# CIN head on one core: M's tile rows read ahead of chunk 4, chunk 4's loads and products threaded between the last two, and the first pair's operands ahead of two weight sums

## The chip, the cores and the metric

The kernel runs on one core of one Trainium2 chip. The metric is the device time of one launch in microseconds (us). All data are float32.

## The reference

A compressed interaction network (CIN) with three layers over x of shape (B, F, E) = (1024, 64, 16), pooled over E and reduced to one number per batch row:

```python
x0 = h = x; xs = []
for i in range(3):                       # W0, W1, W2: 128 output channels each
    z = einsum('bfe,bge->bfge', x0, h)   # all products of two features
    y = einsum('oc,bce->boe', W[i], z.reshape(B, -1, E)) + b[i][None, :, None]
    x_i, h = (y[:, :64], y[:, 64:]) if i < 2 else (y, y)
    xs.append(x_i)
out = concatenate(xs, axis=1).sum(axis=2) @ fc_w.T + fc_b     # (1024, 1)
```

The output is linear in the last layer, so the kernel never forms layer 2 (or the kept half of layer 1) in full. It contracts W2 with fc_w beforehand, and with W1 it builds a small matrix, called M in this text, that maps products of x with x to a weighted sum.

## The kernel before

**Tiling.** The batch is cut into 32 chunks of 32 rows; a chunk is x transposed to features on partitions and N = 32*16 = 512 columns. The host lays out two copies: `xa` (128 partitions, four shifted windows, 1 MB a chunk) and `xb` (four tiles of 256 KB, `xb[c][0..3]`, each a shift of the features). A *product* `z[c, j] = xa[c] * xb[c][j]` (128 x 2048) holds four of the 16 tiles of all pairs of features; the index j is called the tile row. 16 tiles, t = 4j + i, times the matching weight tiles `w_all[:, t]` give one chunk's result in PSUM. `w_all[:, t, 0:64]` are the layer-0 weights (from W0), `w_all[:, t, 64:128]` the M weights.

**Where M comes from.** `m_sb` is computed on TensorE, written to a DRAM scratch tile `md` (L428 to L434), and read back skewed: `read_rows` (L479) and `read_columns(j)` (L473) fill the block `ms`, and `q_weights(j)` (L506, VectorE) adds the two parts into `w_all` for tile row j. A column read is made of 256-byte pieces.

**Order of the head.** Chunks 2, 3, 0, 1 (in this order) form the head. `half_contract` (L262) makes their layer-0 half while M is under way. Then `head_q_tile` (L280) multiplies chunks 0 and 1 with the M weights: 16 tiles in order of t, so tile rows j = 0, 1, 2, 3 in turn. After that TensorE contracts chunk 4 (16 tiles) and chunk 5 (14 of 16), does some small matmuls on squares and sums of x (`v0x`, `h_extra`, `q_extra`), and enters the pairs.

**Pairs.** From chunk 6 on, chunks go in pairs (12 of them, `NPAIR`), each pair with fewer matmul tiles by a Winograd-like scheme. Its operands are `B22`, `T3`, `X`, `B21` (VectorE products, `w_product`, L657), `w_both` (L663, adds two xb tiles), and `T2` and its successors (GpSimd differences, `w_mix`, L672). They use weight sums `ws` (L524 to L529) which are made from `w_all` on GpSimd and ScalarE. The window of a pair begins on TensorE with `alpha` from X and `delta` from T3.

**Lists and queues.** Every engine runs its instructions in program order. From L537 on, the program order is that of a list: `at(when, fn, ...)` records a call, and the list is sorted by `when` at the end (one unit is about one TensorE tile of 0.86 us; `when = 0` is chunk 4's first tile, `t = T0 = 33` the first pair's window). Before the change everything up to L534, the whole of `head_q_tile` among it, stands ahead of that list. `load_xa`, `load_xb` issue from the SyncE queue (SPq). Each xb tile that VectorE multiplies is first copied into PSUM by ScalarE (`second`, L577; two banks, tag "y"). GpSimd multiplies three products itself with xb from SBUF: (4, 3), (5, 2), (5, 3). `weigh`, `add_up`, `place` (L560, L564, L569) scale W1's and W0's kept halves by fc_w on GpSimd, sum them on VectorE and put the columns in place on ScalarE. Fourteen blocks `z0..z13` are handed out in the order in which they came free (`take`, `used`).

A DMA signals one of a few semaphores; before one of these is used again, the earlier DMA on it must have landed.

Of the kernel before, what the change touches and what calls it, by code (L numbers as in the profile page):

```python
# [38 lines left out]
AF = mybir.ActivationFunctionType  # L39
ALU = mybir.AluOpType  # L40
# [10 lines left out]
NI = 4  # L51
NJ = 4
NT = NI * NJ
# [4 lines left out]
KEPT = HEAD[-2:]  # L58
NV = 200
SQ = slice(96, 128)  # L60
# [8 lines left out]
def cin_kernel(ctx, tc, xra, xrb, wh, w0r, w1h, w2t, wx1, wx0, vec, out):  # L69
    nc = tc.nc  # L70
# [6 lines left out]
    halves = [slice(0, F), slice(F, 128)]  # L77

    def const_tile(name, shape):
        return const.tile(shape, F32, tag=name, name=name)  # L80
# [4 lines left out]
    def take(uses=1):  # L85
        n = vacant.pop(0)
        left[n] = uses
        return n

    def used(n, times=1):  # L90
        left[n] -= times
        assert left[n] >= 0
        if left[n] == 0:
            vacant.append(n)
# [9 lines left out]
    w0ds, fcr = vs[:, 8:72], vs[:, 72:200]  # L104
# [25 lines left out]
    w_all = const_tile("w_all", [128, NT, 128])  # L130
    ws = const_tile("ws", [128, 5, 2 * NI, F])
    va, vb, v0 = (const_tile(n, [128, F]) for n in ("va", "vb", "v0"))
# [8 lines left out]
    def load_xa(c, at=slice(0, NI)):  # L141
        if c not in xas or at.start == 0:
            xas[c] = xp.tile([128, NI, N], F32, tag="xa", name=f"xa_{c}")
        nc.sync.dma_start(
            out=xas[c][:, at, :],
            in_=bass.AP(
                tensor=xra.tensor, offset=c * XR * N + at.start * N,
                ap=[[N, 128], [1, (at.stop - at.start) * N]],
            ),
        )  # L150

    def quarter(c, j):
        xbs.setdefault(c, {})[j] = xp.tile([128, N], F32, tag="xb", name=f"xb_{c}_{j}", bufs=9)
        return xbs[c][j]

    def load_xb(c, *js):
        for j in js or range(NJ):
            nc.sync.dma_start(out=quarter(c, j), in_=xrb[c, :, j, :])
# [74 lines left out]
    def new_acc(c, n=N, tag="acc"):  # L233
        if c == NCH - 1:
            parts[c] = [
                (ps.tile([128, cols.stop - cols.start], F32, tag=tag, name=f"acc_{c}_{n}", bufs=bufs), cols)
                for n, (tag, bufs, cols) in enumerate(
                    (("acc", 4, slice(0, E * CUT)), ("set", 2, slice(E * CUT, N)))
                )
            ]  # L240
            return
        accs[c] = ps.tile([128, n], F32, tag=tag, name=f"acc_{c}", bufs=4 if tag == "acc" else 2)
# [34 lines left out]
    def head_q_tile(k, j, i):  # L277
        t = j * NI + i
        for c in (2 * k, 2 * k + 1):
            nc.tensor.matmul(  # L280
                accs[c][halves[1 - c % 2]], w_all[:, t, 64:128], blocks[zs[c, j]][:, i, :],
                start=(t == 0), stop=False, skip_group_check=True,
            )
            used(zs[c, j])
# [97 lines left out]
    for h in range(2):  # L382
        at = slice(32 * h, 32 * h + 32)
# [38 lines left out]
    def m_ap(f1, f2, dims):  # L422
        return bass.AP(tensor=md.tensor, offset=md.offset + f1 * row + f2 * F, ap=dims)
# [12 lines left out]
        in_=m_rows[0:4, 4 * F :].rearrange("p (k c) -> p k c", c=4 * F),  # L436
    )
    used(mb)
    load_xa(4, slice(0, 2))

    for j in (0, 1):
        xb3 = ps.tile([128, N], F32, tag="y", name=f"xp_{c3}_{j}")
# [18 lines left out]
    msb = take()  # L461
    ms = flat(msb).rearrange("p (v t g) -> p v t g", v=2, g=F)

    def skewed(f1, f2, dims):

        at = len(dims) - 2
        return m_ap(f1, f2, dims[:at] + [[row + F, F]] + dims[at:])
# [4 lines left out]
    def read_columns(j, queue, half):  # L472
        queue.dma_start(  # L473
            out=ms[halves[half], 1, j * NI : (j + 1) * NI],
            in_=skewed(0, 16 * half + 4 * (j + 1), [[row, NI], [1, F]]),
        )

    def read_rows(js, queue, half):
        queue.dma_start(  # L479
            out=ms[halves[half], 0].rearrange("p (j i) g -> p j (i g)", i=NI)[:, js],  # L480
            in_=skewed(
                16 * half + 4 * (js.start + 1), 0, [[4 * row, js.stop - js.start], [1, NI * F]]
            ),
        )

    for half, queue in enumerate(queues):
        read_rows(slice(0, 1), queue, half)
        read_columns(0, queue, half)
        read_rows(slice(1, NJ), queue, half)
    load_xa(4, slice(2, NI))  # L490


    new_acc(c3, H2)
# [2 lines left out]
    keep_h1(c2)  # L496
    half_contract(c3, 0, 3, 1, 2, last=2)

    for j in range(1, NJ):
        for half in range(2):  # L500
            read_columns(j, nc.scalar if half and j == 2 else nc.sync, half)
    nc.sync.dma_start(out=va[halves[1]], in_=m_ap(0, 0, [[row + F, F], [1, F]]))

    def q_weights(j):
        at = slice(j * NI, (j + 1) * NI)
        nc.vector.tensor_tensor(w_all[:, at, 64:128], ms[:, 0, at], ms[:, 1, at], ALU.add)  # L506
# [2 lines left out]

    for j in range(NJ):
        q_weights(j)
    used(msb)
    nc.vector.memset(w_all[SQ, (NJ - 1) * NI, 64:128], 0.0)


    load_xb(4)
    for c in KEPT:
        new_acc(c, tag="set")  # L520
    for t in range(NT):
        head_q_tile(0, t // NI, t % NI)

    nc.gpsimd.tensor_tensor(ws[:, 2], w_all[:, 0:8, 0:64], w_all[:, 0:8, 64:128], ALU.subtract)  # L524
    nc.gpsimd.tensor_tensor(ws[:, 1], ws[:, 0], w_all[:, 0:8, 64:128], ALU.add)
    nc.gpsimd.tensor_tensor(ws[:, 3], w_all[:, 8:16, 64:128], ws[:, 1], ALU.subtract)
    nc.gpsimd.tensor_tensor(vb[halves[1]], va[halves[1]], w0ds[halves[1]], ALU.subtract)
    nc.scalar.activation(ws[:, 4], w_all[:, 8:16, 0:64], AF.Identity, scale=-1.0)
    nc.scalar.activation(ws[:, 4, NI], ws[:, 2, NI], AF.Identity, scale=-1.0)  # L529

    cst = const_tile("cst", [128, 1])

# [6 lines left out]
    def at(when, fn, *args, **flags):  # L539
        ops.append((when, len(ops), fn, args, flags))  # L540
# [39 lines left out]
    def plain_product(when, c, j):  # L580
        at(when - 2.6, second, c, j)
        at(when, product, c, j, uses=NI)
# [193 lines left out]
    def load_pair(t, p, b0, a0, b1, a1):  # L776
        a, b = p["a"], p["b"]
        at(t + b0, load_xa, b)
        at(t + b0, load_xb, b, 2, 0)
        at(t + a0, load_xa, a)  # L780
        at(t + a0, load_xb, a, 0)
        at(t + b1, load_xb, b, 3, 1)
        at(t + a1, load_xb, a, 1, 2, 3)
        for c in (b, a):
            at(t + 1, load_e, c)
            at(t + 14, square, c)
        at(t + 1.1, load_xx, p["k"])


    T0 = 33  # L790
    at(-7, load_chunk, 5)
    at(-0.2, load_wx, 0, wx0)
    at(-0.1, load_wx, 1, wx1)
    at(-1.5, copy_x, 4)
    at(4.5, copy_x, 5)
    for v, fc, mul, add, put in ((0, fcr[:, 0:64], 4, 17, 17.1), (1, fcr[:, 64:128], 5, 20, 20.1)):
        at(mul, weigh, v, fc)
        at(add, add_up, v)
        for vw in (va, vb) if v else (v0,):
            at(put, place, v, vw, QS if v else 1.0)  # L800
    for j in range(NJ - 1):
        plain_product(-6.5 + 3 * j, 4, j)
    for j in range(2):
        plain_product(4 + 2.6 * j, 5, j)
    for when, c, j in ((-6, 4, 3), (2, 5, 2), (3, 5, 3)):
        at(when, product, c, j, engine=nc.gpsimd, uses=NI)
    for k in (0, 2):
        at(-0.6, new_y, k, "acc")
# [14 lines left out]
    for c in (4, 5):  # L823
        at(T0 + 19.5, factors, c)
    at(T0 + 19.6, sums, 2, slice(0, 128), slice(0, 1))


    pairs = []
    for n in range(NPAIR):
        k = n + 3  # L830
        s = k % 2
        p = {
            "k": k, "A": halves[s], "O": halves[1 - s], "b": 2 * k + s, "a": 2 * k + 1 - s,
            "late": 1 + n % 2 if n else 0,
        }
        pairs.append(p)
        t = T0 + SPAN * n
        if n == 0:
            load_pair(t, p, -39.9, -33.3, -33.15, -27)
            make_pair(  # L840
                t, p, (-23.4, -20.7, -20.4, -17.8, -14.2, -11.5, -8.1, -7, -4, 3),
                (-5, -4.9, 7.2, 12.4, 16.4, 21.7),
            )
            left5 = [[(contract_half, 5, 3, i, n) for i in (2, 3)] for n in range(2)]
            window(
                t, p, ([left5[1][0], (q_extra, 4, va)], [left5[1][1]]),
                [left5[0][0], (q_extra, 5, va), None, None], [left5[0][1], None],
                GROUPS,
            )
        else:  # L850
            q = pairs[-2]
            load_pair(t, p, -34, -28, -27.8, -27.7)
            make_pair(
                t, p, (-21.4, -18.7, -18.4, -15.8, -12.2, -9.5, -6.1, -2, 1.6, 4.2),
                (-5, 2.8, 7.2, 12.4, 16.4, 21.7),
            )
            window(t, p, (first_fill(q), second_fill(q)), late_run(q))
            end_pair(t, q, (0.7, 11.7, 17.9, 22.3, 23.2, 24, 27.5))
# [45 lines left out]
    c, k = NCH - 1, NP - 1  # L904
    t, q = T0 + SPAN * NPAIR, pairs[-1]
    for n, when in ((2, t - 34), (3, t - 29), (c - 1, t - 12), (c, t - 3)):
# [150 lines left out]
```

## Time and profile before

| | |
|---|---|
| median of 5 runs | 468.26 us (464.82 to 470.85) |
| the profiled execution | 468.26 us, of which 466.5 us are the span from the first to the last instruction |
| granted TensorE clock, mean | 0.996 |
| TensorE busy | 457.1 us (98%) |
| VectorE busy | 398.4 us (85%) |
| GpSimd busy | 330.3 us (71%) |
| ScalarE busy | 119.1 us (26%) |
| DMA | 86.04 MB, 184 GB/s over the span |

In a timeline line the columns are: start in us, length in us, engine, line of the kernel, operation, output<-input, the count of merged instructions, and in brackets the idle time of the engine just before, with what ended it. In the chain of waits a line is start, length, and what the end of the program was waiting for at that moment. PE is TensorE, DVE VectorE, ACT ScalarE, POOL GpSimd, SPq the queue of SyncE. TensorE records two matmuls for each float32 matmul, 0.43 us each at 512 columns.

### The profile page before, as it was taken

To read this page: it belongs to the slowest core of one execution; us is meant where nothing else is said; L and a number is where in the kernel's file an instruction comes from. 1 tells how busy PE (TensorE), PEld (TensorE's weight loads), DVE (VectorE), ACT (ScalarE), POOL (GpSimd) and SP (SyncE) were. 2 spreads that over 40 slices of the span, in tenths; PEclk is the share of its full clock that TensorE was granted. 3 is DMA by queue.
4 is the path that set the end of the run, shared out by engine and by line. 5 is a ranking of instruction groups with operands and counts; after the bars stand their busy time and mean duration, and the time that the engine had idled before them with its cause. 6 is when DMAs were issued, how large, how long until landed. Compare 5 with 4: busy or idle time off the path is not lost.

```text
span 466.5 us, 6048 instructions
## 1 busy us (share of the span) xinstructions
PE 457.1 (98%) x2308; PEld 169.0 (36%) x2308; DVE 398.4 (85%) x283; ACT 119.1 (26%) x219; POOL 330.3 (71%) x99
## 2 busy tenths in 40 slices
PE   7999899998999999999999999999999999999997
PEld 4565243332333333333333333333333333244444
DVE  4994897999798989989898998989898998999621
ACT  2162331241313113131213113131312214222111
POOL 5322789596898979899798979899798979500000
PEclk9999999998999999999999999999999999999999
DMA  7998896393728174553719274472818565061000
GB/s 300 415 288 223 284 413 259 138 299 123 262 53 307 58 250 155 181 215 129 278 35 301 83 242 162 141 253 91 288 44 281 165 204 191 16 210 36 0 0 2
DMA packets 32752, 86.04 MB, mean 184 GB/s; under 512 B 6128, under 2 KB 6800, under 8 KB 27924
## 3 DMA queue, kind: packets, MB, share of 16 engines
q1 hardware_dynamic: 31668, 84.64, 53.0%
q10 hardware_dynamic: 1056, 1.02, 0.9%
q8 instruction: 18, 0.29, 0.2%
q14 instruction: 10, 0.08, 0.1%
HBM read 84.00 MB, written 1.64 MB: 184 GB/s over the span
## 4 chain that ended last, share of the span: by engine, by line
PE 90%; DMA 4%; DVE 2%; SPq 2%; issue 1%; ACT 1%; ACTq 0%; DVEq 0%
PE alpha L549 53%; PE acc L549 16%; PE delta L549 8%; PE beta L549 7%; PE acc L262 2%; PE acc L280 2%; DMA z<-md 2%; DMA z<-in_w0r 2%; DVE z L657 1%; DMA md<-z 1%; PE y L549 1%; SPq L433 1%; SPq L432 0%; PE pm L399 0%; PE pv L372 0%
## 5 line engine op out<-in xcount | busy, mean ns | idle before, releaser
L672 POOL TENSOR_TENSOR z<-z,z 128x2048 f32<-128x2048 f32 x72 | 286.6, 4016 | 38.0 <-PE alpha L549 32.8
L657 DVE TENSOR_TENSOR z<-xa,xp 128x2048 f32<-128x2048 f32 x96 | 216.7, 2280 | 15.3 <-POOL z L672 13.7
L549 PE MATMUL alpha<-z,ws 128*64 128x512 f32 x576 | 196.6, 593 | 0.0
L549 PE MATMUL delta<-z,ws 128*64 128x512 f32 x336 | 152.2, 600 | 0.0
L577 ACT COPY xp<-xb 128x512 f32<-128x512 f32 x93 | 54.6, 588 | 207.2 <-DVE z L657 170.3
L549 PEld LDWEIGHTS alpha<-z,ws 128*64 128x64 f32 x576 | 61.6, 137 | 106.1 <-issue 105.9
L549 PE MATMUL beta<-z,w_all 128*64 128x512 f32 x216 | 96.9, 593 | 0.0
L549 PE MATMUL alpha<-z,w_all 128*64 128x512 f32 x192 | 88.6, 605 | 2.2 <-DVE z L657 2.0
L549 PE MATMUL acc<-z,w_all 128*64 128x512 f32 (+3 forms) x320 | 77.2, 509 | 0.0
L248 DVE TENSOR_TENSOR z<-xa,xp 128x2048 f32<-128x2048 f32 (+2 forms) x33 | 67.6, 2087 | 4.3 <-ACT xp L577 1.6
L549 PEld LDWEIGHTS delta<-z,ws 128*64 128x64 f32 x336 | 45.1, 138 | 9.1 <-issue 9.1
L549 PEld LDWEIGHTS alpha<-z,w_all 128*64 128x64 f32 x192 | 25.8, 139 | 61.3 <-issue 49.5
L549 PEld LDWEIGHTS acc<-z,w_all 128*64 128x64 f32 (+1 forms) x320 | 32.3, 148 | 35.8 <-issue 35.4
L549 PEld LDWEIGHTS beta<-z,w_all 128*64 128x64 f32 x216 | 29.0, 137 | 14.0 <-issue 14.0
L262 PE MATMUL acc<-z,w_all 128*64 128x256 f32 x256 | 29.1, 382 | 1.9 <-DVE z L248 1.7
L248 POOL TENSOR_TENSOR z<-xa,xb 128x2048 f32<-128x2048 f32 x4 | 18.2, 4558 | 16.4 <-DMA xb<-in_xrb 16.4
L262 PEld LDWEIGHTS acc<-z,w_all 128*64 128x64 f32 x256 | 17.9, 137 | 14.2 <-DVE z L248 3.6
L549 PE MATMUL delta<-z,w_all 128*64 128x512 f32 x48 | 22.6, 592 | 0.0
L298 DVE SCALAR_TENSOR_TENSOR uu<-acc,vs,snap 64x512 f32<-64x512 f32 (+2 forms) x5 | 3.2, 643 | 20.1 <-ACT snap L291 20.1
L307 DVE TENSOR_REDUCE acc<-uu 128x64 f32<-128x1024 f32 (+3 forms) x20 | 20.2, 1016 | 0.2
L663 DVE TENSOR_TENSOR xp<-xp,xb 128x512 f32<-128x512 f32 x24 | 16.8, 698 | 0.7
L179 ACT ACTIVATE e<-e 64x512 f32<-64x512 f32 x28 | 16.1, 621 | 4.1 <-DMA e<-in_xra 3.9
(101 smaller groups left out, 297.5 us busy)
## 6 DMA issues: line engine op xcount, KB each, us to landing
xb<-in_xrb SPq DMA_DIRECT2D x128, 256.0 KB, 6.8
xa<-in_xra SPq DMA_DIRECT2D x31, 1024.0 KB, 5.3
e<-in_xra SPq DMA_DIRECT2D x28, 128.0 KB, 4.1
xx<-in_xra SPq DMA_DIRECT2D x28, 128.0 KB, 2.5
z<-in_w2t SPq DMA_DIRECT2D x2, 1024.0 KB, 10.8
z<-in_wx SPq DMA_DIRECT2D x2, 1024.0 KB, 9.4
xa<-in_xra SPq DMA_DIRECT2D x3, 512.0 KB
z<-in_w1h SPq DMA_DIRECT2D x1, 1024.0 KB
```

The source lines that it names most:

```text
L179: nc.scalar.activation(es[c][halves[1]], es[c][halves[0]], AF.Square)
L248: engine.tensor_tensor(blocks[zs[c, j]][:, at, :], xas[c][:, at, :], xbs[c][j].unsqueeze(1).to_broadcast([128, last - first, N]), ALU.mult,)
L262: nc.tensor.matmul(accs[c][halves[n]], w_all[:, t, 0:64], blocks[zs[c, j]][:, i, n * H2 : (n + 1) * H2], start=(t == 0), stop=(j == last a ...
L280: nc.tensor.matmul(accs[c][halves[1 - c % 2]], w_all[:, t, 64:128], blocks[zs[c, j]][:, i, :], start=(t == 0), stop=False, skip_group_chec ...
L298: nc.vector.scalar_tensor_tensor(uu[h, 0, cols], acc_c[h], bh1[h], q, ALU.add, ALU.mult)
L307: nc.vector.tensor_reduce(acc[rows, of, k, half], uu[rows, of if at is None else at, E * half.start : E * half.stop].rearrange("p k (b e) ...
L433: nc.sync.dma_start(out=m_ap(64, 64, [[row, 32], [1, 4 * F]]), in_=m_rows[0:32, 0 : 4 * F])
L549: nc.tensor.matmul(out, w, rhs, start=start, stop=stop, skip_group_check=True)
L577: nc.scalar.copy(bank, xbs[c][j])
L657: nc.vector.tensor_tensor(blocks[b], xas[c], xbs[c][j].unsqueeze(1).to_broadcast([128, NI, N]), ALU.mult)
L663: nc.vector.tensor_tensor(bank, bank, xbs[p["b"]][j], ALU.add)
L672: nc.gpsimd.tensor_tensor(blocks[o][:, tiles], blocks[x][:, tiles], blocks[y][:, tiles], ALU.subtract)
```

## The change

- Chunk 4's `xa` is no longer loaded in two halves around the reads of M's rows. It is loaded whole after the column reads of tile row 1, followed by xb 3 and xb 0, the column reads of row 2, xb 1, the column reads of row 3, the read for `va`, and xb 2. All column reads of rows 1 to 3 go to SyncE's queue; one of them was on ScalarE's.
- `q_weights(2)`, `q_weights(3)`, `head_q_tile`, the weight sums (`w_sums`) and chunk 4's products become entries of the sorted list. On VectorE the order is q_weights 0, 1, product (4, 0), q_weights 2, product (4, 1), q_weights 3 and its memset, product (4, 2). On GpSimd it is the first two weight sums, product (4, 3), the rest of the weight sums. TensorE's own order is as before.
- Chunk 5's first VectorE and its two GpSimd products, and the copies of chunks 4 and 5, get earlier entries in the list.
- For the first pair, B22 and T3 of the second row, the sum between them, and X of the second row move ahead in the list: the first three stand before both `add_up`, X just after them (before the change: the first ahead of the second `add_up`, the rest after it). Its two T2 differences on GpSimd move from 28 and 28.1 in the list to 19 and 20.6; they still follow both `weigh` calls.

```diff
-    load_xa(4, slice(0, 2))                      # after the writes of M
...
-    load_xa(4, slice(2, NI))                     # after read_rows
...
-    for j in range(1, NJ):
-        for half in range(2):
-            read_columns(j, nc.scalar if half and j == 2 else nc.sync, half)
+    for half in range(2):
+        read_columns(1, nc.sync, half)
+    load_xa(4)
+    load_xb(4, 3, 0)
+    for half in range(2):
+        read_columns(2, nc.sync, half)
+    load_xb(4, 1)
+    for half in range(2):
+        read_columns(3, nc.sync, half)
     nc.sync.dma_start(out=va[halves[1]], in_=m_ap(0, 0, [[row + F, F], [1, F]]))
+    load_xb(4, 2)
...
-    for j in range(NJ):
+    for j in range(2):
         q_weights(j)
-    used(msb)
-    nc.vector.memset(w_all[SQ, (NJ - 1) * NI, 64:128], 0.0)
-    load_xb(4)
-    for c in KEPT:
-        new_acc(c, tag="set")
-    for t in range(NT):
-        head_q_tile(0, t // NI, t % NI)
...
+    def last_q_weights():
+        q_weights(NJ - 1)
+        used(msb)
+        nc.vector.memset(w_all[SQ, NT - NI, 64:128], 0.0)
+    def w_sums(m):     # the six weight sums of before, the first two in m = 0
...
+    for c in KEPT:
+        at(-17, new_acc, c, tag="set")
+    for m in range(NT):
+        at(m - 16, head_q_tile, 0, m // NI, m % NI)
+    at(-11, q_weights, 2)
+    at(-7, last_q_weights)
+    at(-16, w_sums, 0)
+    at(-6.9, w_sums, 1)
+    for j, when in enumerate((-12.3, -10.5, -6)):
+        plain_product(when, 4, j)
...
-    at(-1.5, copy_x, 4)
-    at(4.5, copy_x, 5)
+    at(-7, copy_x, 4)
+    at(1, copy_x, 5)
...
-    for j in range(NJ - 1):
-        plain_product(-6.5 + 3 * j, 4, j)
     for j in range(2):
-        plain_product(4 + 2.6 * j, 5, j)
-    for when, c, j in ((-6, 4, 3), (2, 5, 2), (3, 5, 3)):
+        plain_product(-3 + 2.6 * j, 5, j)
+    for when, c, j in ((-12, 4, 3), (-2, 5, 2), (-1, 5, 3)):
         at(when, product, c, j, engine=nc.gpsimd, uses=NI)
...
             make_pair(
-                t, p, (-23.4, -20.7, -20.4, -17.8, -14.2, -11.5, -8.1, -7, -4, 3),
-                (-5, -4.9, 7.2, 12.4, 16.4, 21.7),
+                t, p, (-23.4, -20.7, -20.4, -17.8, -17.2, -16.8, -16.6, -12.5, -4, 3),
+                (-14, -12.4, 7.2, 12.4, 16.4, 21.7),
```

More of the change, by code (lines that the diff above doesn't have):

```diff
@@ L508, in cin_kernel @@
     keep_h1(c3)
-    for j in range(NJ):
+    for j in range(2):
         q_weights(j)
-    used(msb)
-    nc.vector.memset(w_all[SQ, (NJ - 1) * NI, 64:128], 0.0)
-    load_xb(4)
-    for c in KEPT:
-        new_acc(c, tag="set")
-    for t in range(NT):
-        head_q_tile(0, t // NI, t % NI)
[L524 to L529, printed above, removed]
     cst = const_tile("cst", [128, 1])
@@ L787, in load_pair @@
         at(t + 1.1, load_xx, p["k"])
+    def last_q_weights():
[3 more added lines that the diff above has]
+    def w_sums(m):
+        h, q = w_all[:, 8 * m : 8 * m + 8, 0:64], w_all[:, 8 * m : 8 * m + 8, 64:128]
+        if m:
+            nc.gpsimd.tensor_tensor(ws[:, 3], q, ws[:, 1], ALU.subtract)
+            nc.gpsimd.tensor_tensor(vb[halves[1]], va[halves[1]], w0ds[halves[1]], ALU.subtract)
+            nc.scalar.activation(ws[:, 4], h, AF.Identity, scale=-1.0)
+            nc.scalar.activation(ws[:, 4, NI], ws[:, 2, NI], AF.Identity, scale=-1.0)
+            return
+        nc.gpsimd.tensor_tensor(ws[:, 2], h, q, ALU.subtract)
+        nc.gpsimd.tensor_tensor(ws[:, 1], ws[:, 0], q, ALU.add)
+    for c in KEPT:
[8 more added lines that the diff above has]
+        plain_product(when, 4, j)
     T0 = 33
```

## The prediction

> **What bounds the kernel now.** I read first the busy shares and TensorE's waits, then the chain of waits around the two places that the diff touches, then VectorE, GpSimd and the clock in those stretches.
>
> ```profile
> PE 457.1 (98%) x2308; PEld 169.0 (36%) x2308; DVE 398.4 (85%) x283; ACT 119.1 (26%) x219; POOL 330.3 (71%) x99
> ...
> PE alpha L549 <- DVE z L657: 2.0, 1, 2.0
> PE acc L262 <- DVE z L248: 1.7, 1, 1.7
> PE acc L280 <- DVE w_all L506: 1.6, 1, 1.6
> ```
>
> TensorE sets the time. Of its idle time only two pieces lie where the change works: 1.65 us before tile row 1 of M in `head_q_tile`, and 2.03 us before the second pair. The chain shows the first:
>
> ```profile
> 39.41 5.96 DMA z<-md
> 45.37 0.02 issue
> 45.38 2.19 DMA z<-md
> 47.58 0.01 issue
> 47.59 0.44 DVE w_all L506
> 48.02 0.04 issue
> 48.07 10.52 PE acc L280 x48
> 58.59 0.54 PE pc L890 x4
> ```
>
> Reads of M's rows that were issued at 39.4 land at 45.37; `q_weights(1)` runs at 47.59 though the first column read of row 1 went out at 40.70. Just ahead of that read SPq issues half of chunk 4's xa (40.06, 512 KB). Rows 2 and 3 are then already there: 10.52 us for three tile rows, 3.5 us each. The second place, and the clock after each gap:
>
> ```profile
> 113.63 0.64 PE L549 MATMUL alpha<-z,w_all 128*64 128x512 f32 x1 [2.03 <-DVE z L657]
> ...
> 45.99:49.40 3.41, 1.76 (x9) 0.49 (x8) 1.81 (x3) 0.00 (x0) 1.31 (x1) 1.00 0.36 87
> 110.84:114.26 3.42, 1.39 (x12) 0.34 (x6) 3.39 (x3) 1.18 (x2) 1.21 (x1) 1.00 0.55 196
> 114.26:117.67 3.41, 3.41 (x12) 0.98 (x8) 3.38 (x3) 0.59 (x1) 0.00 (x0) 0.50 0.87 290
> ```
>
> The first figure after the length is TensorE's busy time, the third from the right its clock. A stretch of 3.41 us with 1.76 us busy left the clock at 1.00; one with 1.39 us was followed by 3.41 us at 0.50, which cost another 1.7 us. So the second gap costs 3.7 us, the first 1.65; 5.4 us (1.2%) is all there is to win here.
>
> The third thing to see is how VectorE and GpSimd meet in the head:
>
> ```profile
> L506 DVE TENSOR_TENSOR w_all<-z x4: 417/425/1491, 41.7 to 48.3; 128x256 f32<-128x256 f32 x4
> ...
> 47.59 2.17 DVE L506 TENSOR_TENSOR w_all<-z 128x256 f32<-128x256 f32 x3 [5.50 <-DMA z<-md]
> ...
> 48.09 1.38 POOL L524 TENSOR_TENSOR ws<-w_all 128x512 f32<-128x512 f32 x1 [10.41 <-DVE w_all L506]
> 49.44 1.45 POOL L525 TENSOR_TENSOR ws<-ws,w_all 128x512 f32<-128x512 f32 x1
> ...
> 54.12 4.56 POOL L248 TENSOR_TENSOR z<-xa,xb 128x2048 f32<-128x2048 f32 x1 [1.44 <-DMA xb<-in_xrb]
> ```
>
> Of the `q_weights` adds, three take 0.42 us, the last 1.49: it began at about 48.3, after GpSimd's sum of 48.09, and ended at 49.8, just after that sum.
>
> **What the Trainium skill says.** "SBUF — State Buffer", Who interferes with whom: a VectorE instruction with two SBUF inputs and a GpSimd instruction that reads SBUF exclude each other for the whole instruction. The 1.49 us add agrees (both inputs in SBUF); products with xb in PSUM keep 2.2 to 2.3 us beside GpSimd. "TensorE: Matmul & The Clock Gate", Part 1: the clock is judged over free-running windows of 3413 ns and halves after an idle one. The trace agrees on the length, but a window with 1.39 us of work was idle enough. "DMA: Bandwidth & Descriptors", Queues, rings and completion order: each DMA engine takes descriptors in ring order. The column reads behind xa agree.
>
> **The change, part by part.** Sums are against the profiled execution: 468.26 us, span 466.5, which is also the median, so nothing is to be converted.
>
> *Row 1.* The two halves of xa 4 (1 MB) no longer stand among the reads. An M read alone went from issue (38.54) to use (41.67) in 3.1 us; the second read of row 1 now goes out at about 40.7, so it lands at 43.8; 45.4 at the latest, if the row reads land no earlier than now. I take `q_weights(1)` at 45.0. TensorE ends row 0 at 46.42. The 1.65 us go, with 1 us to spare.
>
> *Chunk 4 in the middle.* SPq now issues xa 4 at about 41.5, xb 3 and xb 0, and then the reads of row 2. 1 MB + 256 KB at 400 GB/s (the rate of 56 to 62 us) are 3.3 us, starting when the reads ahead have drained, about 43.5; with 0.7 us to the signal (an estimate from the read of 45.38: 2.2 us to landing, 0.6 of them its issue, the rest start, data and signal) xb 3 is there at 47.5 and xb 0 at 48.2. Row 2's reads follow at about 49.3 and row 3's at 50.9: before, they were there by 48. The read moved from ACT's queue to SPq costs one issue of 0.6 us, hidden in the transfer ahead.
>
> *Row 2's add.* TensorE needs it at 46.42 + 3.5 = 49.9. VectorE has product (4, 0) ahead of it: xb 0 at 48.2, ScalarE's copy 0.6, product 2.3, so 51.1. GpSimd makes the first two sums from 45.5 (1.38 + 1.45, to 48.3) and then product (4, 3), 4.56 us, to 52.9. The add reads two SBUF operands, so at 51.1 it finds GpSimd busy and waits: 52.9 + 0.3 = 53.2. TensorE starts row 2 at 53.25: idle 3.35 us where before it was 1.65, so +1.7 from the wait itself. Bounds for the start: 51.65 if nothing excludes the add, 54 if the first sums start 0.8 us later. Behind the waiting add on VectorE stand product (4, 1), row 3's add and (4, 2): 53.2 + 2.3 + 0.5 + 2.3 = 58.3, against 57.9 now. Row 3's add, at 55.9, meets no GpSimd work, since `w_sums(1)` waits for it, and row 3 is due after 56.7.
>
> *Clock.* The window 49.40 to 52.81 (on the grid seen above) has about 0.5 us of work, so TensorE is at half speed until 56.2: (56.2 - 53.25)/2 = 1.5 us. Ends: 0 if the windows fall otherwise, 1.7 at full. Head end 53.25 + 7.0 + 1.5 = 61.75, against 58.59: **+3.15 us**.
>
> *Chunks 4 and 5.* TensorE has 24 us of work there, now shifted by 3.15. (4, 1) and (4, 2) are done 8 and 7 us before they are due; GpSimd's (5, 3) ends at 57.5 + 9.1 = 66.6, against 67.9 now. SPq's later loads come as now: pair 1's first xa waits for (4, 2), 58.3 for 57.9. The scratch blocks handed out earlier are ones long free. ScalarE's moved copies cost nothing (26% busy).
>
> *First pair ahead of the sums.* Now VectorE idles 2.71 us at 70.9 for GpSimd's `weigh` and ends X's second row at 85.9. With the pair's products ahead of `add_up` that wait is filled, and X's second row ends at about 83.2. But next on VectorE stands `x_v0x`, which needs TensorE's `y`: those matmuls run at 83.35 to 85.3, shifted to 86.5 to 88.4. So VectorE, which now reaches `x_v0x` at 85.84 just as `y` is ready, will wait, and the lead over TensorE shrinks to about 1.2 us. In the second pair's first product it shrinks again: ScalarE's copy for it stands behind the snaps of `alpha` and `delta` (94.06 and 94.67) and ends at 95.74, where VectorE begins at 96.36: 0.6 us of lead is left. Everything after is back to back to 113.6. So the gap before the second pair falls from 2.03 to 1.4 us: -0.6. The window then holds 2.0 us of work, more than the 1.76 that kept the clock: -1.7. GpSimd's T2, after `weigh` as before, is ready some 4 us sooner; TensorE does not wait for it now, so nothing is won there. **-2.3 us**.
>
> Later pairs: no gap of TensorE in the trace of before, all work the same: 0.
>
> Sum: +3.15 - 2.3 = +0.85 us; 468.26 + 0.85 = **469.1 us**. With the bounds above (start of row 2 from 52.5 to 54, clock 0 to 1.7, the second gap's clock kept or not) 466.5 to 471.5 in this case.
>
> **Rivals.** *The add slips through, and the change does what it says.* Chunk 4's tiles land about 1 us sooner, and the add runs at once after (4, 0): row 2 at 50.4 to 51.65, idle 0.5 to 1.75, clock kept: head end 57.4 to 58.65, which is -1.2 to +0.05, and with -2.3: 464.8 to 466.0, say 465.5. For it: DMA moves only 78 GB/s from 46 to 49 us, so there is room. Against it: the 1.49 us add, and GpSimd's 4.56 us product just where row 2 is due.
>
> *Chunk 4's loads are the bound (slower).* If the DMA delivers xa 4 at the 256 GB/s of 43 to 46 us rather than at 400, that is 1.9 us more, 2.2 with small reads beside it: (4, 3) starts at 50.5, row 2 at 55.4. From about 54.7 on a second window (52.8 to 56.2) has too little work, and half speed lasts to 59.6, 2.1 us in all. Head end 64.5: +5.9, and with -2.3: 471.9. For it: the reads of 256 bytes among the 2 KB and 8 KB ones; against: all 8 KB transfers from 53 us on reach 380 GB/s or more.
>
> *The second gap stays.* VectorE's lead is used up wholly, and the half clock comes there too: +3.15 to +3.7, 471.6. For it: both holds named above leave 0.6 us of 2.7; against: nothing is added to VectorE after `x_v0x`.
>
> **How the numbers follow.** Forecast 0.45, slip-through 0.25, loads 0.20, gap stays 0.10. The likeliest gives 469.1. For 8 in 10, from the lower part of the slip-through case with its loads early (464) to the loads case with a further microsecond (473). One per cent, 4.7 us, is about what a measurement of this kernel can tell from no change: faster by more needs nearly all of the 5.4 us, 0.08 from the second case; slower by more (above 472.9) comes from the loads case (0.10) and the ends of the other two (0.05); same 0.77.
>
> **What would show it.** In the changed profile: no wait of TensorE before row 1; one of about 3.3 us before row 2, ended by `w_all` L506 on VectorE; that L506 lasting well over 0.42 us, to just after the end of GpSimd's (4, 3) at about 53; clock 0.50 for one window there and none near 114 to 118; VectorE idle before L303; the wait before the second pair at 1.4 us. Wrong it would be if row 2's add took 0.42 us beside GpSimd, if xb 0 landed by 47, or if the second pair had no wait.

## The result, and the profile after

The changed kernel takes 470.94 us (median, 469.07 to 472.45) against 468.31 us for the kernel before: a ratio of 1.0057, 95% interval [1.0043, 1.0071]. That is 2.6 us slower and inside one per cent, as forecast; 469.1 us was predicted, 464.0 to 473.0 as the range. The profiled execution took 471.1 us, with a span of 469.3 us where before it was 466.5.

TensorE's longest wait in the changed kernel (total, how often, longest), and the chain through the head (start, length, what was waited for):

```profile
PE acc L280 <- DVE w_all L511: 4.3, 1, 4.3
...
46.18 6.32 DMA z<-md
52.51 0.03 issue
52.53 0.02 DVEq L511
52.55 0.94 issue
53.49 0.86 DVE w_all L511
54.35 0.04 issue
54.40 9.68 PE acc L280 x32
64.07 0.54 PE pc L904 x4
```

(L511 is `q_weights`, L506 before.) The wait of 1.65 us before tile row 1 is gone. In its place stands one of 4.26 us before row 2. Two tile rows then take 9.68 us where two had taken 7.0, so the head ends at 64.07 instead of 58.59. The chain as printed goes through a column read that lands at 52.51, but that is the last read of row 3; the signals in the trace show row 2's two reads complete at 50.91 and 51.09. What held the add of row 2 is seen on VectorE, ScalarE and GpSimd (timelines of the changed kernel):

```profile
45.12 0.42 DVE L511 TENSOR_TENSOR w_all<-z 128x256 f32<-128x256 f32 x1 [3.14 <-DMA z<-md]
51.29 2.29 DVE L248 TENSOR_TENSOR z<-xa,xp 128x2048 f32<-128x2048 f32 x1 [5.74 <-ACT xp L566]
53.49 0.85 DVE L511 TENSOR_TENSOR w_all<-z 128x256 f32<-128x256 f32 x1
...
50.61 0.59 ACT L566 COPY xp<-xb 128x512 f32<-128x512 f32 x1 [6.35 <-DMA xb<-in_xrb]
...
49.54 4.52 POOL L248 TENSOR_TENSOR z<-xa,xb 128x2048 f32<-128x2048 f32 x1 [1.36 <-DMA xb<-in_xrb]
```

VectorE was idle for 5.74 us for ScalarE's copy of chunk 4's xb 0, which waited for the DMA until 50.61. Product (4, 0) then ran ahead of row 2's add, and the add (0.85 us) began at 53.49, only 0.6 us before GpSimd's product ended at 54.06. So when TensorE ran out of work at 50.14, row 2's reads were 1 us away, and the product cost the add another 2.4 us. The clock (stretch, length, busy time of TensorE and of the other engines, then TensorE's clock third from the right):

```profile
49.40:52.81 3.41, 0.73 (x4) 0.00 (x0) 1.52 (x1) 1.18 (x2) 3.27 (x1) 1.00 0.95 246
52.81:56.23 3.42, 1.83 (x6) 0.60 (x8) 3.42 (x3) 2.58 (x5) 1.25 (x1) 0.50 0.81 288
56.23:59.64 3.41, 3.41 (x12) 0.95 (x10) 3.31 (x5) 1.38 (x4) 1.99 (x3) 0.50 1.07 427
59.64:63.05 3.41, 3.41 (x19) 1.10 (x17) 3.41 (x2) 2.23 (x4) 3.41 (x1) 1.00 1.02 406
```

Two stretches at half speed follow the start of the wait, 52.81 to 59.64, and TensorE works in them from 54.40: (59.64 - 54.40)/2 = 2.6 us. This is one execution: of 39 of the changed kernel 22 have a mean clock of 0.992 or 0.993 like this one (median 471.3 us), 17 one of 0.996 (470.0), which is what one stretch at half speed gives. The second place, and VectorE ahead of it:

```profile
89.97 1.61 DVE L303 SCALAR_TENSOR_TENSOR uu<-y,cx,xx 128x512 f32<-128x512 f32 x2 [4.79 <-PE y L538]
...
118.52 0.64 PE L538 MATMUL alpha<-z,w_all 128*64 128x512 f32 x1 [1.44 <-DVE z L646]
```

VectorE waits 4.79 us for TensorE's `y`, the wait before the second pair is 1.44 us (2.03 before), and no half clock follows it. The sum: +5.5 in the head, -0.6 and -1.7 at the second pair, +3.2 us; the last run of 96 matmuls starts 3.2 us later in the chain (457.09 for 453.89), and the span grows by 2.8; the other 0.4 us were won after those matmuls, which is not explained.

### The profile page after: what moved, and what is told of

The parts are those of the page before. It is cut to its first block, busy times and chain, and to the rows that moved or that the text cites. A ratio compares the mean times of both kernels' runs of the same rounds, so it can differ in the third digit from the quotient of the medians.

```text
span 469.3 us, 6049 instructions
## 1 busy us (share of the span) xinstructions
PE 458.1 (98%) x2308; PEld 169.2 (36%) x2308; DVE 397.8 (85%) x283; ACT 118.9 (25%) x219; POOL 330.0 (70%) x99
## 4 chain that ended last, share of the span: by engine, by line
PE 92%; DMA 3%; DVE 2%; issue 1%; SPq 1%; ACT 0%; DVEq 0%; ACTq 0%
PE alpha L538 53%; PE acc L538 15%; PE delta L538 7%; PE beta L538 7%; PE acc L262 6%; PE acc L280 2%; DMA z<-in_w0r 2%; DMA z<-md 1%; DVE z L646 1%; PE y L538 1%; PE pv L372 0%; SPq L472 0%; PE pm L399 0%; DVE uu L298 0%; SPq L144 0%
## 5 line engine op out<-in xcount | busy, mean ns | idle before, releaser
L538 PE MATMUL delta<-z,ws 128*64 128x512 f32 x336 | 150.5, 594 | 0.0
L538 PE MATMUL alpha<-z,w_all 128*64 128x512 f32 x192 | 86.9, 595 | 1.6 <-DVE z L646 1.4
L538 PEld LDWEIGHTS alpha<-z,w_all 128*64 128x64 f32 x192 | 25.4, 137 | 59.4 <-issue 48.2
L280 PE MATMUL acc<-z,w_all 128*64 128x512 f32 x64 | 16.7, 683 | 4.3 <-DVE w_all L511 4.3
```

The source lines that it names most:

```text
L280: nc.tensor.matmul(accs[c][halves[1 - c % 2]], w_all[:, t, 64:128], blocks[zs[c, j]][:, i, :], start=(t == 0), stop=False, skip_group_chec ...
L538: nc.tensor.matmul(out, w, rhs, start=start, stop=stop, skip_group_check=True)
```

## The experiments

Ratios are to the kernel before, timed anew beside each group of runs (medians 467.16 to 468.59 us), with 95% intervals. Waits and timelines are those of one profiled execution each.

**The first pair's order alone.**

```diff
 # the kernel before
-                t, p, (..., -17.8, -14.2, -11.5, -8.1, -7, -4, 3),
-                (-5, -4.9, 7.2, 12.4, 16.4, 21.7),
+                t, p, (..., -17.8, -17.2, -16.8, -16.6, -12.5, -4, 3),
+                (-14, -12.4, 7.2, 12.4, 16.4, 21.7),
```

> The kernel before with only the first pair's new order. Theory: VectorE gains 2.7 us, is held by TensorE's y and by ScalarE's snaps, and 0.6 us of lead is left: the wait before the second pair falls from 2.0 to 1.4 us and the clock stays at full speed there; head as before. Some 2.3 us faster, ratio 0.995. Rival: in the changed kernel that wait fell because TensorE came 5 us later, and the order of the first pair alone does nothing: wait 2.0 us, one stretch at half clock, ratio 1.000.

Measured: 465.6 us, ratio 0.9952 [0.9928, 0.9976]. One line of VectorE and two of TensorE in its timeline:

```profile
84.29 1.61 DVE L303 SCALAR_TENSOR_TENSOR uu<-y,cx,xx 128x512 f32<-128x512 f32 x2 [1.97 <-PE y L549]
...
47.87 10.52 PE L280 MATMUL acc<-z,w_all 128*64 128x512 f32 x48 [1.18 <-DVE w_all L506]
...
112.84 0.64 PE L549 MATMUL alpha<-z,w_all 128*64 128x512 f32 x1 [1.44 <-DVE z L657]
```

The theory's numbers: 1.44 us at the second pair, VectorE held at L303 by `y`, mean clock 0.999. This part of the change, on its own, is a gain of 0.5%, some 2.3 us. (The wait before row 1, which this edit does not touch, is 1.18 us here and was 1.65 before: by so much can one execution differ from another.)

**All of the change but that order.** The reverse edit in the changed kernel.

> The changed kernel with the first pair's order of before. Theory of the prediction (the two parts add up): head as in the changed kernel, wait before the second pair back at 2.0 us with half clock after it, 2.3 us slower than the changed kernel, ratio to before 1.0106. Rival: TensorE is so late after the head that VectorE has its lead anyway, so the order adds nothing here: wait 1.4 us, ratio 1.0057 as the changed kernel.

Measured: 471.03 us, ratio 1.0066 [1.0044, 1.0088]; VectorE at L303, and the wait before the second pair:

```profile
90.80 1.61 DVE L303 SCALAR_TENSOR_TENSOR uu<-y,cx,xx 128x512 f32<-128x512 f32 x2 [4.08 <-PE y L538]
...
119.35 0.64 PE L538 MATMUL alpha<-z,w_all 128*64 128x512 f32 x1 [1.44 <-DVE z L646]
```

The rival held: with TensorE 5 us later, VectorE has its lead with either order, and no half clock follows the wait. VectorE was free for L303 at 86.7, no earlier than before (85.84), but TensorE's `y` came 5 us later, so the lead is TensorE's delay and not the earlier products on VectorE. So the two parts do not add up. In the changed kernel the new order of the first pair is worth nothing that these runs can see, and the lead that ends the second gap's half clock comes from the delay in the head.

**The clock.** Matmuls whose result nobody uses, placed in TensorE's wait.

```diff
 # the changed kernel
+    def fill_clock():
+        idle = ps.tile([128, N], F32, tag="acc", name="idle", bufs=4)
+        for _ in range(15):
+            nc.tensor.matmul(idle[:, 0:128], zeros, zeros, start=True, stop=True)
+    at(-8.05, fill_clock)
```

> The changed kernel with 15 matmuls of zeros into an unused PSUM tile (3.2 us) between tile rows 1 and 2 of the head, where TensorE waits 4.3 us. Theory: the wait is the same, but the clock does not fall, which saves (59.6 - 54.4)/2 = 2.6 us: head end at 61.5, ratio to before 1.000. Rival: the half clock does not come from that wait, or costs nothing because something else is late: ratio 1.0057.

Measured: 468.66 us, ratio 1.0014 [0.9994, 1.0034]; TensorE in the head:

```profile
43.23 7.04 PE L280 MATMUL acc<-z,w_all 128*64 128x512 f32 x32
55.88 7.09 PE L280 MATMUL acc<-z,w_all 128*64 128x512 f32 x32 [2.06 <-DVE w_all L511]
```

Although row 2 starts 1.5 us later in this execution, two rows take 7.1 us again instead of 9.7, at a mean clock of 0.999. The medians differ by 2.3 us, close to the 2.6 expected: of the 5.5 us that the head loses in the profiled execution, nearly half is the clock.

**GpSimd's product out of the way.**

```diff
 # the changed kernel
-    for when, c, j in ((-12, 4, 3), (-2, 5, 2), (-1, 5, 3)):
+    for when, c, j in ((-6.8, 4, 3), (-2, 5, 2), (-1, 5, 3)):
```

> The changed kernel with GpSimd's product (4, 3) after the last weight sums, so no GpSimd work lies beside row 2's add. Theory after the result: chunk 4's loads set the add's start, exclusion costs 0.43 us: L511 falls from 0.85 to 0.42, TensorE's wait from 4.3 to 3.8 us, ratio 1.005. The forecast's own step (GpSimd holds the add, loads are early): wait falls to 1.75 us, ratio 0.996.

Measured: 470.23 us, ratio 1.0038 [1.0021, 1.0056].

```profile
54.03 0.42 DVE L511 TENSOR_TENSOR w_all<-z 128x256 f32<-128x256 f32 x1
```

The add falls to 0.42 us as both theories say, but it still begins at 54.03, when product (4, 0) is done; TensorE's wait is 4.62 us in this execution, so the 3.8 expected was not seen. The median is 0.7 us below the changed kernel's, and the two intervals overlap. Exclusion is not what sets the start of row 2.

**Row 2's add first, with and without that product.**

```diff
 # the changed kernel; in the second, also the edit above
-    at(-11, q_weights, 2)
+    at(-12.4, q_weights, 2)
```

> The changed kernel with row 2's add ahead of product (4, 0) on VectorE; GpSimd's (4, 3) where it was. If a two-SBUF-input add and GpSimd's product exclude each other: the add starts at 51.1, when row 2's reads have landed, and lasts 3.2 us, to the end of (4, 3) at 54.1; TensorE's wait stays at 4.2 us, ratio 1.006. If they do not: the add takes 0.42 us, the wait is 1.7 us, ratio 0.995.

> The same with GpSimd's (4, 3) after the last weight sums. Theory: the add runs at the landing of row 2's reads, 51.1, in 0.42 us; TensorE waits 1.7 us before row 2, the clock holds or falls for one stretch; 3 to 5 us less than the changed kernel, ratio 0.995 to 0.999. Rival: something else (row 3's reads, which land at 52.7, or chunk 4's products, now later) takes the wait over: ratio 1.003 or more.

Measured: 470.53 us, 1.0058 [1.0034, 1.0082], and 466.97 us, 0.9978 [0.9961, 0.9996]. VectorE and GpSimd of the first, then VectorE of the second:

```profile
49.77 3.23 DVE L511 TENSOR_TENSOR w_all<-z 128x256 f32<-128x256 f32 x1 [5.03 <-DMA z<-md]
...
48.21 4.51 POOL L248 TENSOR_TENSOR z<-xa,xb 128x2048 f32<-128x2048 f32 x1 [0.83 <-DMA xb<-in_xrb]
```

```profile
50.48 0.42 DVE L511 TENSOR_TENSOR w_all<-z 128x256 f32<-128x256 f32 x1 [5.93 <-DMA z<-md]
```

This settles the exclusion: the same add, its data in place, takes 3.23 us beside a GpSimd product and ends at 53.0, 0.3 us after it (48.21 + 4.51 = 52.7); without the product it takes 0.42. TensorE's wait is 3.4 us in the first kernel (4.2 expected; the reads landed 1.3 us sooner than expected in this execution). The Trainium skill's rule ("SBUF — State Buffer", Who interferes with whom) holds here with its full price. Only with both edits does it fall to waits that leave the clock at 1.00, one before row 2 and one before row 3, whose add now stands behind two products:

```profile
50.96 3.65 PE L280 MATMUL acc<-z,w_all 128*64 128x512 f32 x16 [1.34 <-DVE w_all L511]
55.88 3.65 PE L280 MATMUL acc<-z,w_all 128*64 128x512 f32 x16 [1.26 <-DVE w_all L782]
```

**The loads: which of them are slow.** The column reads of rows 2 and 3 and `va` behind all of chunk 4's loads (called the unmixed kernel below).

> The changed kernel with the column reads of rows 2 and 3 and va behind all of chunk 4's loads. If those reads, taken up among the loads, are what slows xb 0 (it landed at 50.5, forecast 48.2): ScalarE's copy of xb 0 starts at 48.5 to 49, VectorE's product (4, 0) at 49.5. If the loads themselves are slower than 400 GB/s here: the copy stays at 50 to 51. Row 2's add waits for its reads in both cases, at 51 or later, so the time is not better than the changed kernel's.

Measured: 469.88 us, ratio 1.0056 [1.0034, 1.0079].

```profile
51.13 0.59 ACT L563 COPY xp<-xb 128x512 f32<-128x512 f32 x1 [6.68 <-DMA xb<-in_xrb]
```

The copy of xb 0 is no earlier (51.13; 50.61 in the changed kernel). So the 256-byte reads among the loads are not what delays them; those of row 1, which go out ahead of xa in both kernels, were not moved here. The completion signals say more: in the changed kernel the 16 DMA engines report xb 0 between 47.53 and 50.53, so the first is there as forecast and the last 3.0 us later, and the last decides. It is 2.8 us in the unmixed kernel, but 0.6 us in the kernel of the next experiment, whose loads go out behind all column reads. Why the engines drift apart is left open.

**All column reads ahead of chunk 4, and both adds ahead of its products.**

```diff
 # the changed kernel
-    for half in range(2):
-        read_columns(1, nc.sync, half)
-    load_xa(4)
-    load_xb(4, 3, 0)
...
-    load_xb(4, 2)
+    for j in range(1, NJ):
+        for half in range(2):
+            read_columns(j, nc.scalar if half and j == 2 else nc.sync, half)
+    nc.sync.dma_start(out=va[halves[1]], in_=m_ap(0, 0, [[row + F, F], [1, F]]))
+    load_xa(4)
+    load_xb(4, 3, 0, 1, 2)
...
-    at(-11, q_weights, 2)
-    at(-7, last_q_weights)
+    at(-12.5, q_weights, 2)
+    at(-12.4, last_q_weights)
```

> The changed kernel with all column reads and va ahead of chunk 4's loads (xa, xb 3, 0, 1, 2), and rows 2 and 3's adds ahead of product (4, 0). Theory: no wait in the head (rows 1 to 3 in place by 47), head end 57; product (4, 0) about 53, still ahead of its use at 57; second gap 1.4 us with full clock: 1.65 + 0.6 + 1.7 = 4 us less than before, ratio 0.9915. Rival: the loads, now 2 us later, make TensorE wait at chunk 4 or VectorE late at the second pair: ratio 0.996 to 1.002.

Measured: 463.91 us, ratio 0.9912 [0.9878, 0.9947], below both kernels. The whole head is one piece of TensorE's timeline; under it row 3's add and the first products of chunk 4 and 5 on VectorE:

```profile
43.06 13.90 PE L280 MATMUL acc<-z,w_all 128*64 128x512 f32 x64
...
46.25 0.76 DVE L506 TENSOR_TENSOR w_all<-z 128x256 f32<-128x256 f32 x1 [0.65 <-DMA z<-md]
52.34 11.08 DVE L248 TENSOR_TENSOR z<-xa,xp 128x2048 f32<-128x2048 f32 x5 [5.14 <-ACT xp L561]
```

The last add is done at 47.0. Chunk 4's first product, begun at 52.34, is 2.3 us ahead of its use at 57. What the change had right is loading xa after the reads of row 1; what costs time is putting it ahead of the reads of rows 2 and 3, together with product (4, 0) ahead of row 2's add. This kernel undoes both at once and does not say how much each is worth.

**What holds the second pair at 1.44 us.** In the kernel of the last experiment, ScalarE's copy for the second pair's first product 0.6 units earlier in the list (`p["k"] > 3` for `> 4` in `make_pair`), then also the copy for the second row of B22.

> The kernel with all column reads ahead of chunk 4's loads, and the second pair's first copy on ScalarE 0.6 units earlier in the list, ahead of the snaps of alpha and delta, as the later pairs have it. Theory: the wait of 1.44 us before the second pair is the same in five kernels because that copy stands behind the snaps; ahead of them VectorE starts its product 0.5 to 0.6 us sooner, and the wait falls to 0.7 to 0.9 us: ratio to before 0.990. Rival: the lead is lost again at the next copy behind a snap (that of the second row), and the wait stays at 1.4 us: ratio 0.9912.

> The kernel before this one (first copy of the second pair ahead of the snaps) with the copy for the second row of B22 ahead of the snap of alpha + bias as well. Theory: with the first copy moved alone the wait stayed at 1.44 us, as the second copy stands behind a snap that waits for TensorE, and VectorE runs back to back from its end to X, 9.9 us later. With both ahead, VectorE keeps its lead of about 1.2 us: the wait falls to 0.7 to 0.9 us, ratio 0.990. Rival: a third hold (the snap of chunk 5 for L298, which needs TensorE's last tile of chunk 5) keeps the wait at 1.2 us or more: ratio 0.991.

Measured: 463.79 us, 0.9913 [0.9882, 0.9945], and 464.19 us, 0.9915 [0.9888, 0.9941]; waits of 1.4 us in the first and 1.5 us in the second, whose snap also made TensorE wait another 0.9 us. Nothing won. There was little to win: in the changed kernel the first copy holds VectorE for 0.48 us (0.47 with the pair's order alone), but in the kernel of the last experiment by less than 0.2 us, because VectorE comes later there itself (it reaches `x_v0x` at 83.47 without a wait for `y`). With that copy moved, the next hold is the copy behind the snap of alpha + bias, and it too is under 0.1 us (three products that take 6.68 us elsewhere take 6.73):

```profile
99.82 0.68 ACT L667 ACTIVATE snap<-alpha,vs 64x512 f32<-64x512 f32 x1 [4.01 <-PE alpha L533]
100.53 0.59 ACT L561 COPY xp<-xb 128x512 f32<-128x512 f32 x1
```

From the end of that copy (101.1) VectorE runs back to back for 9.9 us to X at 111.0. In the second kernel that hold was gone too, but VectorE came to `x_v0x` only at 84.01, having started chunk 4 at about 52, and was simply busy. So 1.4 us is what several limits of about the same size leave: the copies where VectorE comes early, VectorE's own work where it does not.

## Why the prediction was right, and which steps were not

The time was inside the range and the verdict (within one per cent) was the forecast. But the case that came true is nearest to the rival "chunk 4's loads are the bound", which had 0.20 and 471.9 us; the forecast's own case, with 0.45, was too short in two terms, the loads and the clock, and it was in part luck that the total stayed close: the second gap's gain came, but not by the step that was to bring it. By its steps:

- *Row 1*: right. `q_weights(1)` at 45.12, forecast 45.0; no wait.
- *Chunk 4 in the middle*: the term that was mis-sized. xb 0 was put at 48.2 from a rate of 400 GB/s, read at 56 to 62 us; its copy began at 50.61. From 43 to 52 us the changed kernel moved 272 GB/s. The sum also took the 16 engines as one pipe: the first engine's part of xb 0 was there at 47.53, the last one's at 50.53. The rival had named 256 GB/s, seen at 43 to 46 us before, and gave its reason as the 256-byte reads beside the load, which the unmixed kernel did not bear out.
- *Row 2's add*: the start was forecast at 53.25 and was 54.40, by another way. It was to find GpSimd busy from 51.1 to 52.9, 1.8 us of exclusion; in fact product (4, 0) ended at 53.5 and exclusion cost 0.43. The rule was right (3.23 us when the add came first), its share in this kernel wrong; the rival, too, had the add wait for GpSimd.
- *Clock*: one stretch at half speed was counted (1.5 us), there were two (2.6). The rival had set the point from which there are two at a start of about 54.7; they came at 54.40. Both sums asked how long TensorE is busy in a stretch, as if a microsecond at half speed counted like one at full speed; by the traces it does not (last section).
- *First pair*: -2.3 us was met in size (1.44 us of wait for 1.4 forecast; full clock), and alone that order gives some 2.3. But the sum ascribed it to the new order, and with the order undone it stays. The failing step is adding an edit that frees VectorE to one that delays TensorE: the second gives VectorE the same lead. The hold was named as the copy behind the snaps of alpha and delta. It is in the trace (VectorE idle 0.48 us for it), but the copy was moved only in a kernel where it holds VectorE by less than 0.2 us, so what moving it alone is worth here was not tested.
- *Head end* 61.75 forecast, 64.07 measured; *total* +0.85 forecast, +2.6 measured.

## What to carry to other kernels

Where a load is put among small reads that a busy engine waits for, take its rate from that very stretch of the profile and not from the smooth one after it, and remember that the last of the 16 engines decides. Ask which instruction stands ahead of the waiting one on its engine: here the add of row 2 could have run when its reads had landed (51.1), but stood behind a product that began at 51.3. Two edits that each remove the same wait do not add; test each alone. And price a wait of TensorE with its clock: here 1.65 us cost only themselves, 2.03 us cost another 1.7.

## What the runs showed of the hardware

**What keeps the clock.** In the traces the clock changes only at a grid of 3.413 us: it stays at one value for 3.413, 6.827 or 47.787 us, which is 1, 2 or 14 times that. Counted as TensorE's busy time in a stretch of 3.41 us, no single limit fits: 1.76 us at full speed kept it full, 1.83 us at half speed kept it at half, and in the unmixed kernel so did 2.25 us at half speed. Counted as work at full speed, that is busy time times clock, one limit does: 1.83 and 2.25 us at half speed are 0.92 and 1.13 us of work, and a stretch that is busy throughout at half speed holds 1.71. Inside the program, in all traces that record the clock and from its first record on, every stretch with 1.49 us of work or less was followed by half speed (1.39 before the second pair; 1.49 at the end of the kernel with the zero matmuls) and every one with 1.71 or more by full speed. By the limit that this gives, between 1.5 and 1.7 us, a wait of up to 3.41 - 1.71 = 1.70 us costs only itself, and once the clock has halved TensorE must be busy for some 3.0 to 3.4 us of a stretch to get it back, which would be why one long wait can cost two stretches. The limit is fitted to the runs afterwards; none was made to test it.

**One execution and another.** The stretches lie differently against the program in each trace, which would explain why the same wait costs a stretch at half speed in one execution and none in another. Of 58 timed executions of the kernel before, beside the first four experiments, 25 had a mean clock of 0.999 or 1.000 (16 at 1.000, median 466.3 us), 25 had 0.996 (468.4), 3 had 0.995, and 5 were at 0.993 or below (470 to 471). This is a good part of the spread of 6 us between executions of one kernel, but not all: the 16 at 1.000 alone run from 464.9 to 469.4. It is narrower in kernels without the long waits (462.8 to 464.8 us for the one with the column reads first, in 6 runs). With the first pair's new order and a clock of 1.000, 465.6 against 466.3 us leaves 0.7 us for the shorter wait itself, of the 2.4 us between the medians (465.6 and 467.99).
